# Layer 0's q, k, v projections by one level of Strassen's scheme, bias tables fetched for each head, normalising and the residual copy on ScalarE

## The chip, the cores and the metric

The kernel runs on one core of one Trainium2 chip. The metric is the device time of one execution in microseconds. A core has five engines that run beside each other, each with its own queue in order: TensorE (PE; its weight loads are shown apart, as PEld), VectorE (DVE), ScalarE (ACT), GpSimd (POOL) and SyncE (SP), which here only issues transfers.

## The reference, cut to what matters

The input x has shape (T, B, N, D) = (4, 8, 512, 512): T time steps, B images, N tokens and D features. Four layers follow each other, each as x = x + layer(groupnorm(x)). Layers 1 to 3 are convolutions; the change leaves them alone. Layer 0 is spiking attention with H = 8 heads of 64 features:

```python
q = heads(lif(bn(x @ Wq.T, ...)))        # k and v in the same way
scores = einsum('tbhnd,tbhmd->tbhnm', q, k) * scale + bias_table[rel]
out = lif(einsum('tbhnm,tbhmd->tbhnd', scores, v))
out = lif(bn((out * gate_scale + gate_shift) @ Wp.T, ...))
# lif, over t:  v = v + (xt - v) / 2;  spike = v >= 1;  v = v * (1 - spike)
```

There is no softmax, so the kernel takes q (k^T v) for the first part of the scores and multiplies v with a table for each head for the second, where rel depends on n - m alone. All of q, k, v and the outputs are spikes, 0 or 1; x and the weights of the projections are f32.

## The kernel before, in words

**Steps.** layer0 (L254) goes through 32 steps, one for each (image b, time t), with t inside, since lif carries a state over t. Step n computes the projections of its (b, t); in the same pass of the loop (L754) stand the attention and the output projection of steps n - 2 and before. Attention is done for two steps at once, in every second pass.

**Projections.** project_in (L539) makes one 128 x 512 block in one PSUM bank: 4 f32 matmuls over the 4 chunks of 128 features. Each of v, k and q has 4 blocks, so a step has 12 blocks and 48 matmuls. For k and v the tokens are the partitions, for q the features. In the profile an f32 matmul is two instructions. VectorE then takes the block out of PSUM: potential (L511) adds half the state, L553 (k, v) or L502 (q) compares with 1 and writes spikes, L518 or L504 clears what has spiked. The constant of the batch norm is added to the state on GpSimd for v, k and the output projection (L519) and on ScalarE for q (L505). At the last t of an image the state isn't kept.

**The input.** x arrives in four transfers (load_quarters, L454, on SP's queue), is normalised in place by one VectorE operation over 128 x 2048 (L714), and transposed by VectorE in 32 x 32 blocks (L524). The statistics of the next groups are counted from other loads of x (xs, L468).

**Attention.** prepare_bias (L383) builds, once at the start, all tables of the heads in SBUF: 12 transfers with overlapping rows (hankel) on ScalarE's queue, each followed by a reversed ScalarE copy (L398). attend (L580) multiplies the spikes of v with these tables (biased, L590, 144 bf16 matmuls of 256 columns). It splits each table into a part that is shared by both halves of the tokens and two own parts: shared_part, then a ScalarE copy from PSUM to PSUM (L610) onto which own_part accumulates, then copies of halves of the partitions (L622), then q (k^T v) on top (L626) and the lif (neuron_o, L479).

**Output projection.** project_out (L644): ScalarE casts spikes to fp32r (L652), 8 fp32r matmuls (L655), potential, then for each half of the features a VectorE operation that compares and adds the residual x, read with a stride of four elements (L666), and statistics (L670). GpSimd copies the mirrored edges (L677) and starts the store (L682). The residual is loaded on SP's queue (xr, L450).

**What sets the order.** In layer 0 a planner orders each engine's instructions ahead of the run: by the place in the program, by readiness with its own costs, and by free buffers. `issue_after` puts named instructions behind another on its engine. PSUM has 8 banks; 7 (ps_mm) serve the projections, attention and the output projection. Layer 1 starts when the first image's table and rows have been loaded into the space of the weights (start_layer1, L729).

Of the kernel before, what the change touches and what calls it, by code (L numbers as in the profile page):

```python
# [41 lines left out]
ALU = mybir.AluOpType  # L42
# [31 lines left out]
LAG = 2  # L74
RING = W2_N + 2 * LAG + 5
# [6 lines left out]
def shape_constants():  # L82

    p = np.arange(P)
    block = (p[:, None] // DH == p[None, :] // DH).astype(np.float32)
# [168 lines left out]
def layer0(  # L254
# [5 lines left out]
    ps_mm = s.enter_context(tc.tile_pool(name="ps_mm", bufs=7, space=PSUM))  # L260
    ps_1 = s.enter_context(tc.tile_pool(name="ps_1", bufs=1, space=PSUM))
    wpool = s.enter_context(tc.tile_pool(name="w0", bufs=1))


    n_x1 = W1_N * X1_U
    wv = shared.tile([P, NC * D], F32, tag="v", name="w_v")
    wkq = shared.tile([P, max(2 * NC * D, n_x1)], F32, tag="kq", name="w_kq")
    wT = {
        n: w.rearrange("p (c d) -> p c d", c=NC)
        for n, w in (("v", wv), ("k", wkq[:, : NC * D]), ("q", wkq[:, NC * D : 2 * NC * D]))  # L270
    }
    eye = shared.tile([K1_P, SHIFTS, M1], F32, name="eye")


    c_twice = {n: wpool.tile([P, D], F32, name=f"c2_{n}") for n in "vkp"}
    toep = [wpool.tile([P, H, 3, N // 2 + P], BF16, name=f"toep_{j}") for j in range(3)]
# [5 lines left out]
    xp = s.enter_context(tc.tile_pool(name="x0", bufs=4))  # L282
    xqp = s.enter_context(tc.tile_pool(name="xq0", bufs=1))
    small0 = s.enter_context(tc.tile_pool(name="s0", bufs=4))
    x1p = s.enter_context(tc.tile_pool(name="x1p", bufs=2))
    state = s.enter_context(tc.tile_pool(name="state", bufs=1))
    work = s.enter_context(tc.tile_pool(name="work", bufs=1))


    def load_weights(n, engine):  # L290
        rows = i[f"wT_{n}"].rearrange("(q c a) e -> q a c e", c=NC, a=SQ)
        for q in range(P // SQ):
            engine.dma_start(wT[n][q * SQ : (q + 1) * SQ], rows[q])
# [4 lines left out]
    def batch_norms():  # L298
# [13 lines left out]
        )  # L312
        return op.ins

    def as_rows_of(cols, rows):

        n = cols.shape[1]
        ps = ps_mm.tile([n, P], F32, tag="mm", name="ps_rows")
        nc.tensor.transpose(ps, cols, ident)
        nc.scalar.copy(rows[:n], ps)  # L320
        return rows[:n]

    def rows_of():
        return work.tile([P, 2, P], F32, tag="kvb", name="rows", bufs=2)

    def along_free(rows, j):
# [4 lines left out]
        for c in range(NC):  # L331
            at = NC * j + c
            nc.tensor.matmul(
                ps[:, c * P : (c + 1) * P], lhsT=ident[:n, at : at + 1].to_broadcast([n, P]),
                rhs=rows, start=True, stop=True,
            )
# [5 lines left out]
    def prepare_in(n):  # L342
        j = "qkvp".index(n)
        scale = along_free(a_rows, j)
        for k in range(NC):
            nc.vector.tensor_mul(wT[n][:, k, :], wT[n][:, k, :], scale)
        return nc.scalar.mul(c_twice[n], along_free(c_rows, j), 2.0).ins

    n_h, n_u = N - 1, toep[0].shape[3]

    def split_bias():

        parts = tc.dram_tile([3, H * 3 * n_h], BF16, name="bias_parts")
# [13 lines left out]
        nc.vector.tensor_scalar_mul(own, own, math.sqrt(D))  # L367
# [5 lines left out]
        for x in range(3):  # L373
            nc.scalar.dma_start(
                bass.AP(
                    parts.tensor, parts.offset + x * n_h,
                    [[3 * n_h, H], [H * 3 * n_h, 3], [1, n_h]],
# [5 lines left out]
    def prepare_bias(parts):  # L383


        for h in range(0, H, 2):
            for z in range(3):
                hankel = state.tile(
                    [P, 6, n_u], BF16, tag="h_o" if (h + z) % 2 else "h_p", name="hankel"
                )  # L390
                nc.scalar.dma_start(
                    hankel,
                    bass.AP(
                        parts.tensor, parts.offset + (z * H + h) * 3 * n_h,
                        [[1, P], [n_h, 6], [1, n_u]],
                    ),
                )
                nc.scalar.copy(  # L398
                    toep[z][:, h : h + 2].rearrange("p h x u -> p (h x) u"), hankel[:, :, ::-1]
                )  # L400
# [8 lines left out]
    def prepare_out(wp_rows):  # L409
# [5 lines left out]
        for k in range(NC):  # L415
# [19 lines left out]
            nc.scalar.copy(wpT[1][:, k, :], wp)  # L435
        c = c_half[:, 3, :]
# [3 lines left out]
        rows = rows_of()[:, 0]  # L440
        nc.scalar.mul(
            c_twice["p"].rearrange("p (g v) -> p g v", g=PH),
            phases(along_free(as_rows_of(c, rows), 0)), 2.0,
        )
# [48 lines left out]
    def neuron_q(ps, c, t, spikes):  # L493

        a_col, c_col = a_half[:, 0, c : c + 1], c_half[:, 0, c : c + 1]
        h = h_of["q"][:, c, :]
        v = work.tile([P, N], F32, tag="v", name="v_q", bufs=2)
        if t == 0:
            nc.vector.tensor_scalar(v, ps, a_col, c_col, op0=ALU.mult, op1=ALU.add)
        else:  # L500
            nc.vector.scalar_tensor_tensor(v, ps, a_col, h, op0=ALU.mult, op1=ALU.add)
        nc.vector.tensor_scalar(spikes, v, 1.0, None, op0=ALU.is_ge)  # L502
        if t < T - 1:
            nc.vector.scalar_tensor_tensor(v, v, 1.0, v, op0=ALU.is_lt, op1=ALU.mult)  # L504
            nc.scalar.activation(h, v, AF.Identity, bias=c_col, scale=0.5)  # L505

    def potential(ps, n, c, t):

        before = c_twice[n] if t == 0 else h_of[n][:, c, :]
        v = work.tile([P, D], F32, tag="v", name=f"v_{n}", bufs=2)  # L510
        op = nc.vector.scalar_tensor_tensor(v, before, 0.5, ps, op0=ALU.mult, op1=ALU.add)  # L511
        potentials.append(op.ins)
        return v

    def keep(v, n, c, t):
        if t < T - 1:
            h = h_of[n][:, c, :]
            nc.vector.scalar_tensor_tensor(h, v, 1.0, v, op0=ALU.is_lt, op1=ALU.mult)  # L518
            nc.gpsimd.tensor_add(h, h, c_twice[n])  # L519

    def transposed(xt, k):

        xk = work.tile([P, N], F32, tag="xn", name="xn", bufs=5)
        nc.vector.transpose(  # L524
            xk.rearrange("p (j s) -> p j s", s=SQ), xt[:, :, k * SQ : (k + 1) * SQ]
        )
        return xk

    def new_spikes():
# [3 lines left out]
            "q": work.tile([P, NC, 2, N], F16, tag="q", name="q"),  # L533
            "v": work.tile([P, NC, H, 2, DH], F8, tag="vtok", name="vtok"),
            "both": work.tile([P, 2, H, 2, DH], F8, tag="both", name="both"),
# [3 lines left out]
    def project_in(n, c, xn, got, t):  # L539

        ps = ps_mm.tile([P, D], F32, tag="mm", name="ps_in")
        cut = slice(c * P, (c + 1) * P)
        for k in range(NC):
            lhsT, rhs = (wT["q"][:, k, cut], xn[k]) if n == "q" else (xn[k][:, cut], wT[n][:, k, :])
            mm = nc.tensor.matmul(ps, lhsT=lhsT, rhs=rhs, start=k == 0, stop=k == NC - 1)  # L545
        if n == "q":
# [945 lines left out]
```

## Time and profile before

| | us |
|---|---|
| median of 3 runs | 2823.92 |
| lowest, highest | 2821.92, 2826.72 |
| the profiled execution | 2823.14 |
| its span, first to last instruction | 2821.3 |
| first projection matmul of layer 0 | 22.15 |
| first matmul of layer 1's convolution | 1959.36 |

The page of the profile has for every engine the busy time, for every group of instructions (a line, an engine, an operation and its tiles) the count, busy time, mean duration of one in ns, and the idle time just before it with what ended it. A table of stretches gives busy times by window with TensorE's granted clock, the DMA share and GB/s. A timeline gives single instructions with their start and duration in us. Matmuls overlap in the records, so their mean duration is longer than their pace.

| engine, 420 to 660 us | busy us of 240 |
|---|---|
| TensorE | 238.20 |
| VectorE | 197.64 |
| ScalarE | 46.98 |
| GpSimd | 85.67 |

### The profile page before, as it was taken

The page shows a single profiled execution, that of the slowest core. Times are in us where ns is not written, and L with a number is a line of the kernel's source. Part 1 is how long each engine was busy: PE and PEld are TensorE (multiplying, and loading weights), DVE is VectorE, ACT ScalarE, POOL GpSimd, SP SyncE. Part 2 cuts the span into 40 slices and gives each one's busy share as a digit, 9 for nine tenths or more (in the row PEclk, how much of TensorE's full clock was granted, in tenths as well). Part 3 has the DMA queues.
Part 4 walks back from the last instruction along what each step waited for, and adds up shares of the span by engine and source line. Part 5 has one row for each costly group of instructions (what it writes and reads, how often), then busy time and mean ns, then how long its engine had stood idle before and what let it go on. Part 6 is the DMA issues. An engine that isn't in the chain of part 4 may idle for free. (4 is left out here: it accounts for less than half of the span.)

```text
span 2821.3 us, 46325 instructions
## 1 busy us (share of the span) xinstructions
PE 2723.7 (97%) x17558; PEld 1402.5 (50%) x17558; DVE 2061.0 (73%) x3686; ACT 718.0 (25%) x1145; POOL 939.4 (33%) x2144
## 2 busy tenths in 40 slices
PE   7899999999999999999999999999899999789999
PEld 3455555554555555555555555555233333334447
DVE  7787978878788787977878778786565555665550
ACT  1422020221202112022220312202111121366663
POOL 2132433324243242433325324243211111354440
PEclk9899999999999999999999999999999999889999
DMA  6523223232232322323222121113877777667755
GB/s 169 149 77 76 75 71 82 61 76 72 65 91 61 76 69 64 87 61 83 64 65 61 46 69 46 50 63 93 215 204 207 209 214 208 152 177 210 216 170 149
DMA packets 326547, 314.03 MB, mean 111 GB/s; under 512 B 20691, under 2 KB 245771, under 8 KB 326211
## 3 DMA queue, kind: packets, MB, share of 16 engines
q1 hardware_dynamic: 258144, 228.59, 32.6%
q0 software_dynamic: 16448, 51.27, 4.8%
q10 hardware_dynamic: 51731, 31.20, 3.9%
q8 instruction: 138, 2.26, 0.4%
q14 instruction: 86, 0.70, 0.1%
HBM read 207.31 MB, written 103.67 MB: 110 GB/s over the span
## 5 line engine op out<-in xcount | busy, mean ns | idle before, releaser
L545 PE MATMUL ps_in<-w_v,xn 128*128 128x512 f32 x1024 | 465.0, 600 | 13.8 <-DVE xn L524 8.5
L930 PE MATMUL ps_conv<-x,bt 112*64 112x512 f32 x2048 | 449.5, 595 | 17.5 <-DMA x<-x 13.9
L545 PE MATMUL ps_in<-w_kq,xn 128*128 128x512 f32 x1024 | 452.9, 594 | 0.0
L545 PE MATMUL ps_in<-xn,w_kq 128*128 128x512 f32 x1024 | 450.1, 595 | 0.0
L677 POOL COPY x1s<-x1s 128x2 f32<-128x2 f32 (+1 forms) x1024 | 221.5, 271 | 356.8 <-DVE x1s L666 342.7
L545 PEld LDWEIGHTS ps_in<-w_v,xn 128*128 128x128 f32 x1024 | 193.3, 192 | 232.3 <-issue 202.3
L655 PE MATMUL ps_out<-wp,so 128*128 128x512 f32 x1024 | 306.2, 442 | 1.3 <-ACT so L652 1.3
L545 PEld LDWEIGHTS ps_in<-xn,w_kq 128*128 128x128 f32 x1024 | 193.7, 190 | 226.6 <-issue 219.7
L545 PEld LDWEIGHTS ps_in<-w_kq,xn 128*128 128x128 f32 x1024 | 194.4, 190 | 219.4 <-issue 205.9
L930 PEld LDWEIGHTS ps_conv<-x,bt 112*64 112x64 f32 x2048 | 146.6, 136 | 309.7 <-issue 290.6
L652 ACT CAST so<-so 128x512 fp32r<-128x512 fp8e4 x128 | 78.7, 618 | 808.5 <-PE ps_out L655 783.0
L519 POOL TENSOR_TENSOR h_v<-h_v,c_v 128x512 f32<-128x512 f32 x96 | 134.4, 1400 | 449.7 <-DVE h_v L518 326.8
L655 PEld LDWEIGHTS ps_out<-wp,so 128*128 128x128 f32 x1024 | 192.5, 188 | 93.7 <-issue 56.4
L1370 PE MATMUL ps_conv<-x,band_t 32*32 32x512 f32 x6144 | 230.2, 597 | 1.3 <-ACT o L1410 1.3
L666 DVE SCALAR_TENSOR_TENSOR x1s<-v_p,xr 128x256 f32<-128x256 f32 x256 | 180.3, 744 | 17.1 <-DMA x<-x1s 8.4
L937 ACT ACTIVATE xo<-ps_conv,off 128x512 f32<-128x512 f32 x128 | 87.8, 687 | 393.9 <-PE ps_conv L930 329.7
L952 POOL DMA_DIRECT2D x<-xo x128 | 71.6, 566 | 338.0 <-ACT xo L937 329.7
L595 PE MATMUL ps_own<-toep,vtok 128*128 128x256 bf16 x1536 | 180.7, 272 | 3.5 <-ACT ps_own L610 3.5
L1265 DVE SCALAR_TENSOR_TENSOR x<-ps_conv,inv,x 128x512 f32<-128x512 f32 x128 | 95.1, 749 | 103.6 <-PE ps_conv L1229 91.6
L595 PEld LDWEIGHTS <-vtok 128*128 128x128 fp8e4 x1536 | 149.4, 98 | 30.8 <-issue 8.7
L505 ACT ACTIVATE h_q<-v_q,c_half 128x512 f32<-128x512 f32 x96 | 69.2, 721 | 373.3 <-DVE v_q L504 373.3
L519 POOL TENSOR_TENSOR h_k<-h_k,c_k 128x512 f32<-128x512 f32 x96 | 123.8, 1290 | 107.6 <-DVE h_k L518 104.8
(196 smaller groups left out, 3647.0 us busy)
## 6 DMA issues: line engine op xcount, KB each, us to landing
x<-x SPq DMA_DIRECT2D x64, 917.0 KB
x<-x1s POOLq DMA_DIRECT2D x128, 262.0 KB, 2.7
xq<-in_x SPq DMA_DIRECT2D x128, 256.0 KB
xr<-in_x SPq DMA_DIRECT2D x128, 256.0 KB
out<-o SPq DMA_DIRECT2D x120, 256.0 KB
xs<-in_x SPq DMA_DIRECT2D x112, 256.0 KB
x<-x SPq DMA_DIRECT2D x128, 224.0 KB
x<-xo ACTq DMA_DIRECT2D x128, 128.0 KB
```

What stands on the lines that cost most here:

```text
L519: nc.gpsimd.tensor_add(h, h, c_twice[n])
L545: mm = nc.tensor.matmul(ps, lhsT=lhsT, rhs=rhs, start=k == 0, stop=k == NC - 1)
L595: nc.tensor.matmul(out, lhsT=src[:, c, h, :], rhs=toep[z][:, h, x, u : u + half], start=start and c == 0 and z == 0, stop=c == 1 and z == ...
L652: nc.scalar.copy(tokens, so[:, :, t % 2, c * P : (c + 1) * P])
L655: nc.tensor.matmul(ps, lhsT=tokens[:, k, :], rhs=wpT[z][:, k, :], start=k == 0 and z == 0, stop=k == NC - 1 and z == 1,)
L666: nc.vector.scalar_tensor_tensor(own, v.rearrange("p (g v) -> p g v", g=PH)[:, two, :], 1.0, by_phase[:, two, :], op0=ALU.is_ge, op1=ALU.add,)
L677: nc.gpsimd.tensor_copy(x1[:, f, u : u + n], x1[:, fm, um - n + 1 : um + 1][:, ::-1])
L930: mm = nc.tensor.matmul(ps[q * M1 : (q + 1) * M1, :], lhsT=bt[:, z, :], rhs=xt[:, w0 : w0 + N_PS1, z : z + NV], start=z == 0, stop=z == SH ...
L937: nc.scalar.activation(xo[:, a, :], ps, AF.Identity, bias=off[:, t : t + 1])
L952: engine.dma_start(bass.AP(dst.tensor, dst.offset + (q * n_half * W1_OUT * B + b) * D + f * NV, [[B * D, W1_OUT], [W1_OUT * B * D, n_half] ...
L1265: nc.vector.scalar_tensor_tensor(inner, ps, w["inv"], x, op0=ALU.mult, op1=ALU.add, accum_out=sums[:, 0, :] if summed else None,).ins
L1370: mm = nc.tensor.matmul(ps[c * QP : (c + 1) * QP, :], lhsT=band[g * QP : (g + 1) * QP, int(last), dx, :], rhs=src[:, dx : dx + PH, :], sta ...
```

## The change

**Products.** Tokens, features and outputs are each cut in two halves. Instead of 8 products of quarters, 7 products of sums of quarters are made (Strassen's scheme in Winograd's form), and the four result quarters are sums of products. k and v are done together: `unit("kv", cc)` makes blocks of 128 tokens by 256 columns of k and 256 of v; `unit("q", 0)` does q with 256 tokens for two feature chunks. A step has three units: two for k and v, one for q. Sums of products are formed in PSUM: a bank gets a ScalarE copy of another and later products accumulate on it. One product (the seventh) is doubled by ScalarE into SBUF and added to the state on GpSimd.

```diff
+    def product(kind, cc, x, n, ps, start=False):
+        w, x = w_of[n], x[n]
+        for kk in range(2):
+            if kind == "kv":
+                mm = nc.tensor.matmul(
+                    ps, lhsT=x[:, kk, cc * P : (cc + 1) * P], rhs=w[:, :2, kk, :],
+                    start=start and kk == 0, stop=kk == 1, skip_group_check=True,
+                )
+        for c in range(2) if kind == "q" else ():
+            for kk in range(2):
+                mm = nc.tensor.matmul(
+                    ps[:, c, :], lhsT=w[:, 2, kk, c * P : (c + 1) * P], rhs=x[:, kk, :],
...
+        a = new("a")
+        yield mul(a, 1, True)
+        g = new("g")
+        mul(g, 7, True)
+        b = new("b")
+        seeds.append(nc.scalar.copy(b, a).ins)
+        twice = work.tile([P, 2, HN], F32, tag="twice", name="twice")
+        nc.scalar.mul(twice, g, 2.0)
+        for o in range(2):
+            h, c, _ = of(1, o)
+            nc.gpsimd.tensor_add(h, c if t == 0 else h, twice)
+        yield
+        mul(b, 6)
+        yield
+        e = new("e")
+        seeds.append(nc.scalar.copy(e, b).ins)
+        mul(a, 2)
+        evict(a, 0, 0)
+        yield
+        mul(b, 5)
+        yield
+        f = new("f")
+        seeds.append(nc.scalar.copy(f, b).ins)
+        mul(e, 4)
+        evict(f, 1, 1)
+        evict(e, 1, 0)
+        yield
+        mul(b, 3)
+        evict(b, 0, 1)
+        yield
```

**Evictions.** evict adds half the state on VectorE as before. For k and v the threshold is now two operations of 256 columns, which write 2^-6 in place of 1; for q it stays one. GpSimd adds the constant for k and v; for q ScalarE does, in two pieces of 256 columns.

```diff
+            op = nc.vector.scalar_tensor_tensor(
+                v, c if t == 0 and half == 0 else h, 0.5, ps, op0=ALU.mult, op1=ALU.add
+            )
...
+                    nc.vector.tensor_scalar(
+                        out, own, 1.0, SPIKE, op0=ALU.is_ge, op1=ALU.mult, saturate=False
+                    )
...
+                nc.vector.scalar_tensor_tensor(h, v, 1.0, v, op0=ALU.is_lt, op1=ALU.mult)
+                nc.gpsimd.tensor_add(h, h, c)
+            else:
+                nc.vector.scalar_tensor_tensor(v, v, 1.0, v, op0=ALU.is_lt, op1=ALU.mult)
+                for k in range(2):
+                    nc.scalar.activation(
+                        h[:, k], v[:, k], AF.Identity, bias=c_q[:, 2 * o + k : 2 * o + k + 1]
+                    )
```

**Sums of the input and of the weights.** Each step needs four sums of quarters of x, on GpSimd; the weights are summed once at the start, on VectorE, after they have been scaled.

```diff
+    def sum_x(n, part):
+            if part == 0:
...
+                eng.tensor_add(x[5], x[7], x[4])
+                eng.tensor_sub(x[7], x[1], x[7])
+            else:
+                eng.tensor_sub(x[6], x[5], x[1])
+                eng.tensor_sub(x[3], x[2], x[6])
+    def sum_weights(first, end):
...
+        nc.vector.tensor_sub(t3, b22, b12)
+        nc.vector.tensor_sub(t1, b12, b11)
+        nc.vector.tensor_sub(t2, b22, t1)
+        nc.vector.tensor_sub(b12, b21, t2)
```

**Tables.** The tables of all heads no longer lie in SBUF. For each attention the tables are fetched on SP's queue, for each head one shared (128 x 3 x 384 bf16) and one own (128 x 2 x 3 x 384 bf16). Four heads of each kind are held; they are fetched in the pass before, the others as the first come free. The rows come unreversed; instead q and the output spikes are read in reverse.

```diff
+    def fetch(kind, n=1):
+        first, n_x = (0, 1) if kind == "x" else (1, 2)
+        for h in order[kind][:n]:
+            table = tables.tile([P, n_x, 3, n_u], BF16, tag=f"t_{kind}", name=f"table_{kind}")
+            nc.sync.dma_start(
...
+                table = held["x"].pop(0)
+                biased(common[j][:, two, :], both, 2 * j + two, table[:, 0], two == 0)
+            if 2 * j + HEADS_HELD < H:
+                fetch("x", 2)
...
+            if h + HEADS_HELD < H:
+                fetch("own")
```

**Normalising and the residual.** Four ScalarE operations of 128 x 512 normalise x, with r and -m r as columns. In project_out ScalarE copies the residual, by halves, into the output tile, behind the last seed; VectorE then adds in place, contiguously.

```diff
-                nc.vector.tensor_scalar(flat, flat, m, r, op0=ALU.subtract, op1=ALU.mult)
+            for xt in as_rows(xs[n]):
+                nc.scalar.activation(xt, xt, AF.Identity, bias=shift, scale=r)
...
+            with tc.issue_after(seeds[-1]):
+                op = nc.scalar.copy(halves[z][1], by_phase[:, two, :])
...
             nc.vector.scalar_tensor_tensor(
-                own, v.rearrange("p (g v) -> p g v", g=PH)[:, two, :], 1.0,
-                by_phase[:, two, :], op0=ALU.is_ge, op1=ALU.add,
+                own, v.rearrange("p (g v) -> p g v", g=PH)[:, two, :], 1.0, own,
+                op0=ALU.is_ge, op1=ALU.add,
             )
```

**Order.** A step is now a row of 21 slots (7 for each unit). The output projections stand at slots 3, 6, 10 and 13, the normalising of the next step at 13, its transposes at 14 and 17, its sums at 18 and the end, k^T v at 16. The residual's loads stand ahead of the attention, no longer after it. add_halves adds the bytes of two spikes as one 16-bit integer. Seven matmuls with one row of constants are put ahead of everything.

```diff
+    outs = (3, 6, 10, 13)
...
+            if slot == 13 and n <= last:
                 add_halves(spikes, steps[n][1])
+                normalise(n + 1)
+            if slot == 14:
+                transpose(n + 1, 0)
+                if n % 2 == 0 and done >= 0 or n == 1:
+                    fetch("x", HEADS_HELD)
+                    fetch("own", HEADS_HELD)
...
+            if slot == 17:
+                transpose(n + 1, 1)
+            if slot == 18:
+                sum_x(n + 1, 0)
```

## The prediction

> **What bounds the kernel now.** I read the table of stretches first, to see which engine is full while layer 0 runs, and then the groups by cost.
>
> ```profile
> core 0: us, PE busy (x) PEld busy (x) DVE busy (x) ACT busy (x) POOL busy (x), PEclk, DMA share, GB/s
> 420.00:540.00 120.00, 119.55 (x450) 66.38 (x449) 98.49 (x161) 20.89 (x36) 41.66 (x96) 1.00 0.28 74
> 540.00:660.00 120.00, 118.65 (x450) 65.82 (x449) 99.16 (x175) 26.09 (x44) 44.01 (x90) 1.00 0.27 70
> ```
>
> TensorE is busy 99% at full clock, VectorE 82%, ScalarE 20%, GpSimd 36%. Layer 0 is TensorE-bound: only fewer TensorE cycles shorten it, and only until another engine is full. Its work, and what GpSimd does beside it:
>
> ```profile
> L545 PE MATMUL ps_in<-w_v,xn 128*128 128x512 f32 x1024 | 465.0, 600 | 13.8 <-DVE xn L524 8.5
> L545 PE MATMUL ps_in<-w_kq,xn 128*128 128x512 f32 x1024 | 452.9, 594 | 0.0
> L545 PE MATMUL ps_in<-xn,w_kq 128*128 128x512 f32 x1024 | 450.1, 595 | 0.0
> L519 POOL TENSOR_TENSOR h_v<-h_v,c_v 128x512 f32<-128x512 f32 x96 | 134.4, 1400 | 449.7 <-DVE h_v L518 326.8
> ```
>
> An f32 matmul appears as two instructions: 16 matmuls per projection and step, 32 steps, 1024 records. The 600 ns overlap; the pace is read from the weight loads, one for each instruction:
>
> ```profile
> 601.28 0.19 PEld L545 LDWEIGHTS ps_in<-xn,w_kq 128*128 128x128 f32 x1 [0.24 <-issue]
> 601.71 0.19 PEld L545 LDWEIGHTS ps_in<-xn,w_kq 128*128 128x128 f32 x1 [0.24 <-issue]
> 602.14 0.19 PEld L545 LDWEIGHTS ps_in<-xn,w_kq 128*128 128x128 f32 x1 [0.24 <-issue]
> ...
> 641.44 1.70 PEld L655 LDWEIGHTS ps_out<-wp,so 128*128 128x128 f32 x8
> ```
>
> One f32 instruction of 512 columns takes 0.43 us (starts 0.43 apart). Eight fp32r instructions' weight loads of 0.188 cover 1.70: starts (1.70 - 0.19)/7 = 0.216 apart. So a 0.19 us load hides under a 0.216 us matmul. The projections cost 96 x 0.43 = 41.3 us a step. A pair of steps with its attention takes 118.5 us (the projection of v that follows the k,v product starts at 447.80 and at 1751.98, 11 pairs later).
>
> The third reading is VectorE against GpSimd:
>
> ```profile
> 52.38 0.68 DVE L511 SCALAR_TENSOR_TENSOR v_k<-c_k,ps_in 128x512 f32<-128x512 f32 x1
> ...
> 52.55 1.27 POOL L519 TENSOR_TENSOR h_k<-h_k,c_k 128x512 f32<-128x512 f32 x1 [2.01 <-DVE h_k L518]
> 53.10 1.00 DVE L553 TENSOR_SCALAR k<-v_k 128x512 fp8e4<-128x512 f32 x1
> ```
>
> The operation that reads PSUM runs beside GpSimd's addition at 0.68. The threshold after it takes 1.00 where its free time is 0.43: it waits until the addition ends at 53.82.
>
> [...]
>
> **The change, part by part.** The sum is made against the profiled execution: 2823.1 us, its span 2821.3, the other 1.8 taken as constant. It lies 0.8 below the median 2823.92.
>
> *Products.* A unit has 7 products of two 512-column matmuls, or for q of four 256-column ones. Two k-v units: 2 x 7 x 2 x 2 = 56 instructions x 0.43 = 24.1 us. One q unit: 56 instructions of 256 columns; none is in the trace, the nearest row of that length is fp32r's 0.216: 12.1 us. Together 36.2 for 41.3: 5.15 us a step, **165 us** over 32 steps. Bounds of the q pace: half of 0.43 (0.215, nothing gained)[...]. Fully exposed, 0.40, is excluded by the 0.216.
>
> *Seeds.* Products accumulate on copies of earlier ones, so TensorE now waits for ScalarE: three PSUM-to-PSUM copies in a unit, nine a step. Each has one other product, 1.72 us, in between. The same kind of wait is in the trace: ps_x ends at 616.05, ScalarE's copy (L610) runs 616.09 to 616.66, ps_own starts at 616.78; with 0.16 of modelled matmul tail, 0.89 us. So 0.83 us of room: one other ScalarE operation in front (0.4 to 0.8) is covered, two are not. ScalarE has per pair 23.2 now, plus 18 seeds x 0.57, 6 doublings x 0.61, 8 normalisings (0.80 by the page), [...]and q's state in 256-column pieces (12 x 0.49 for 6 x 0.72): 52 us of 108, 48%. Queued behind a late ScalarE operation are the next seed and so TensorE. I take 0.5 us a step, 16 us; ends 0 and 0.4 a seed (115).
>
> *VectorE.* Per pair: normalising leaves, -2 x 1.34; the halves' sum on half the elements, -0.7; the residual addition reads contiguous data, 16 x (0.74 - 0.42) = -5.1; k's and v's thresholds in two pieces, 32 x 0.29 for 16 x 0.43, +2.5. Sum -6.1. GpSimd gets 6 state additions and 4 input sums a step: 320 instructions to the 288 of L519. The 288 cost VectorE now, by mean over free time in three rows, 128 x ((0.998 - 0.426) + (0.616 - 0.426) + (0.668 - 0.427)) = 128 us, 0.45 each. 20 more a pair: +8.9. VectorE goes from 97.6 to 100.4 us, of 108.2 instead of 118.5: 93%. GpSimd: 42.3 + 20 x 1.27 = 68, 63%. Neither exceeds TensorE, but the room for lateness shrinks: a state addition late on GpSimd holds the eviction that reads it, VectorE's queue behind that, and then PSUM banks. I take 0.5 us a step, 16 us; ends 0 and 1.5 (48).
>
> *Tables.* 12 fetches and 12 ScalarE copies (2.11 each) leave the start; each of 16 attentions fetches 8 x (288 + 576) KB = 7.1 MB: 113 MB, about 65 GB/s more on SP's queue, DMA share from 0.28 to about 0.5. Half is held ahead. The other 3.5 MB must come while attention runs, 17.7 us (614.58 to the last ps_own at 632.27). The start's stretch 65:70 moved 338 GB/s, 85:90 292, 60:65 97: at 300 it is 12 us. It fits, with little room, and xr and xq loads share the queue; a fetch that waits for its slot holds those behind it. I take 0.5 us an attention, 8 us; ends 0 and 6 (96).
>
> *The start.* Both k's and v's weights must be scaled and summed ahead of the first full unit[...]; the first product slips from 22.15 to about 25, and waits between the first ones add some us. Against that, TensorE is busy 144 of the 158 us from 22 to 180, with a gap of 5 us at 70 while table fetches fill the DMA; this cover is lighter afterwards. Net 0, ends -10 and +10.
>
> *At nothing:* reversed reads of q and of the spikes (ScalarE's reversed copy L398 moves 2304 elements in 2.11[...]; for the matmul unshown, at worst 8 x 0.35 a pair, 45 us, held unlikely); the shift of the mean (0.2 on VectorE, hidden by its idle time); the added one-row matmuls ahead of the start (TensorE waits for inputs until 22). Layers 1 to 3 (from 1959 on) are untouched.
>
> **Sum.** -165 + 16 + 16 + 8 + 0 = -125; 2823.1 - 125 = 2698. The tails above make it 2658 (no stall) to about 2735.
>
> **Rivals.**
> *Seeds late.* Two ScalarE operations stand in front of many seeds. For: ScalarE's work doubles, in order, with operations that wait for VectorE among it. Against: 48%, and 0.83 us of room. At 0.4 us a seed: 2823 - 165 + 115 + 24 = 2797 with the small terms at what I took; half of it 2740.
> *Tables late.* Attention waits for its last three tables, 6 us each time: 2823 - 165 + 96 + 32 = 2786. For: 17.7 us for 3.5 MB. Against: the prefetch, and 300 GB/s.
> [...]VectorE outgrows TensorE. Without any waits it has 97.6 - 8 - 6.1 = 83.5 us a pair (8 = 128/16); with 38 additions at s each, 83.5 + 38 s. It matches today's 118.5 at **s = 0.92**; beyond, the kernel is slower. At a full lock, 1.27, it is 132 us, 16 x 13.3 = 213 us slower; midway, s = 1.05, 123.4: 16 x 4.9 = +78, 2901. For: GpSimd's additions now come in twos, and most VectorE operations have two SBUF inputs. Against: 0.45 measured, and operations on PSUM and statistics run beside it.
> *The 7/8 isn't had:* q's short matmuls don't halve. Excluded above[...].
>
> **How the numbers follow.** Likeliest case 0.58: 2698 (its own range 2658 to 2740). Seeds late 0.15, tables late 0.10: both still faster.[...] Balance near zero 0.03. About 0.2% (5.6 us) is what a measurement of this kernel can tell from no change. Faster 0.83, same 0.03, slower 0.14. The range from 2658 reaches over the two middle rivals to 2800[...].
>
> **What would show it.** Right: TensorE over 95% busy in layer 0's stretches, a pair near 111 us, q's instructions 0.216 apart, VectorE near 92%, L553's successor with means not far over 0.5. Wrong: waits of matmuls for the seeds' copies (seeds), for DMA (tables), or for VectorE with VectorE over 97%[...]. Layer 1 starting within 10 us of 1959 - 125 = 1834 tests that all of it lies in layer 0.

## The result and the profile after

| | before | after |
|---|---|---|
| median of 4 runs, us | 2823.44 | 2911.61 |
| span of the profiled execution, us | 2821.3 | 2908.5 |
| mean granted TensorE clock | 0.987 | 0.966 |
| TensorE, VectorE, ScalarE, GpSimd busy, us | 2723.7, 2061.0, 718.0, 939.4 | 2656.9, 2142.4, 1166.5, 1319.5 |

The ratio after to before is 1.0315, 95% interval 1.0297 to 1.0334: slower by 88 us, where 125 faster was forecast. All of it lies in layer 0: the first convolution matmul of layer 1 starts at 2060.76, before at 1959.36, 101 later (1834 was forecast), and 14 of those come back afterwards. First the table of stretches, after; its columns are busy us (and instructions) of TensorE, weight loads, VectorE, ScalarE and GpSimd, then granted clock, DMA share and GB/s.

```profile
420.00:540.00 120.00, 110.68 (x470) 72.28 (x469) 99.45 (x173) 49.12 (x86) 63.79 (x109) 0.96 0.47 126
540.00:660.00 120.00, 107.58 (x459) 71.34 (x458) 101.12 (x183) 49.73 (x91) 67.33 (x113) 0.96 0.45 114
```

TensorE fell from 99% to 91% busy, and its clock with it; VectorE stands at 84%, not at the 93% forecast, ScalarE at 41% and GpSimd at 55%. No engine is full. A pair of steps takes 125.0 us (the first product of the second step starts at 583.04 and 11 pairs later at 1958.51) where the prediction counted 108.2 for TensorE's own work. So TensorE waits, in gaps. That q's instructions are not what is slow shows in one of its products (line, operation, count, least, median and longest duration in ns, first and last start):

```profile
L545 PE MATMUL ps_q_b<-x_sum,w_raw x8: 379/379/380, 581.3 to 582.8; 128*128 128x256 f32 x8
```

Eight starts from 581.3 to 582.8, 0.21 apart. In the groups by cost, the projections of k and v have idle time now, where those of before had 0.0 in two of three rows:

```profile
L539 PE MATMUL ps_kv_b<-w_sums,x_sum 128*128 128x512 f32 x512 | 264.6, 643 | 61.6 <-issue 61.1
...
L539 PE MATMUL ps_kv_a<-w_raw,x_raw 128*128 128x512 f32 x512 | 257.5, 622 | 19.8 <-DMA xq<-in_x 9.6
```

The gaps of one pair, from the timeline of TensorE (start, length, the instructions, and in brackets the idle time ahead of them and what ended it):

```profile
574.00 0.55 PE L649 MATMUL ps_kv<-v,k 128*128 128x128 fp8e4 x7 [1.80 <-DVE v L584]
...
583.04 1.88 PE L539 MATMUL ps_kv_a<-w_raw,x_raw 128*128 128x512 f32 x4
585.10 1.98 PE L539 MATMUL ps_kv_g<-w_sums,x_raw 128*128 128x512 f32 x4 [0.18 <-POOL x_raw L851]
591.27 2.96 PE L539 MATMUL ps_kv_b<-w_sums,x_sum 128*128 128x512 f32 x4 [4.18 <-issue]
...
639.66 2.55 PE L671 MATMUL ps_own<-table_own,v 128*128 128x256 bf16 x12 [4.12 <-ACT ps_own L690]
```

Two gaps of over 4 us, one as a step ends and one as attention begins. The label "issue" of the first is a wait of which the profile names no releaser: `ps_kv_b` is a bank that ScalarE seeds with a copy of `ps_kv_a` (L609). `ps_kv_a` was done at 584.9; the copy ran at 590.60, and the matmul followed it at 591.27. What ScalarE did till then, and VectorE and GpSimd with it, is the core of this case. ScalarE first:

```profile
585.63 0.91 ACT L597 ACTIVATE h_q<-v_q,c_q 128x256 f32<-128x256 f32 x2 [5.27 <-DVE v_q L595]
588.78 1.91 ACT L597 ACTIVATE h_q<-v_q,c_q 128x256 f32<-128x256 f32 x4 [2.24 <-DVE v_q L595]
590.60 0.57 ACT L609 COPY ps_kv_b<-ps_kv_a 128x512 f32<-128x512 f32 x1
```

ScalarE idles 5.27 and 2.24 us, waiting for VectorE (L595) with q's state pieces (L597), and the seed stands behind these in its queue. VectorE:

```profile
580.52 3.41 DVE L588 TENSOR_SCALAR q<-v_q 128x512 fp8e4<-128x512 f32 x1
583.96 1.63 DVE L595 SCALAR_TENSOR_TENSOR v_q<-v_q 128x512 f32<-128x512 f32 x1
585.52 0.67 DVE L576 SCALAR_TENSOR_TENSOR v_q<-h_q,ps_q_f 128x512 f32<-128x512 f32 x1
...
587.53 1.15 DVE L595 SCALAR_TENSOR_TENSOR v_q<-v_q 128x512 f32<-128x512 f32 x1
```

A threshold of 0.43 us (L588) takes 3.41, the operation after it 1.63 instead of 0.69. L576, which reads one operand from PSUM, takes its free 0.67. And GpSimd:

```profile
579.15 1.29 POOL L774 TENSOR_TENSOR h_p<-h_p,c_p 128x512 f32<-128x512 f32 x1
580.38 2.04 POOL L614 TENSOR_TENSOR h_q<-c_q,twice 128x512 f32<-128x512 f32 x2
582.37 1.26 POOL L850 TENSOR_TENSOR x_sum<-x_raw 128x512 f32<-128x512 f32 x1
583.71 1.34 POOL L851 TENSOR_TENSOR x_raw<-x_raw 128x512 f32<-128x512 f32 x1
585.01 1.72 POOL L853 TENSOR_TENSOR x_sum<-x_sum,x_raw 128x512 f32<-128x512 f32 x1
586.81 1.33 POOL L854 TENSOR_TENSOR x_sum<-x_raw,x_sum 128x512 f32<-128x512 f32 x1
```

Seven additions all but back to back; six of them the change has added (two of the doubled product, four input sums). VectorE's threshold began at 580.52 and ended at 583.93, after three of them. L595 ended at 585.60, and the addition that began at 585.01 (L853) took 1.72 where L850 took 1.26: it seems that GpSimd can be held as well. Before, nearly all such additions came singly (253 of 255 from 200 to 1900 us), and a threshold of k lost 0.57 on average. And a gap costs more than its length. The same table for two stretches, one ahead of the seed's arrival and one behind it:

```profile
586.00:591.30 5.30, 1.12 (x4) 0.25 (x2) 5.16 (x9) 2.83 (x7) 2.06 (x2) 1.00 0.09 13
591.30:596.00 4.70, 4.70 (x7) 1.95 (x8) 0.29 (x1) 3.12 (x7) 2.49 (x2) 0.64 0.00 0
```

First VectorE works 5.16 of 5.30 us and TensorE 1.12; then TensorE works throughout, at a granted clock of 0.64, and VectorE 0.29. They take turns: an engine with 16% of idle time is what the other waits for. Behind the gap of 4.12 at 639.66 the clock is 0.60 (639.70 to 644.00). It is lower, too, behind the two short gaps of 0.53 and 1.80 us around the k,v product:

```profile
571.00:574.50 3.50, 1.17 (x18) 1.00 (x16) 3.47 (x8) 0.57 (x1) 1.57 (x2) 1.00 0.00 0
574.50:583.00 8.50, 8.50 (x33) 7.19 (x33) 8.46 (x13) 0.57 (x1) 7.37 (x14) 0.80 0.31 81
```

TensorE was busy 1.17 of 3.50 us there, and the clock behind it was 0.80; the matmuls of `ps_q_a` there (574.4 to 576.9) have a median of 0.634 us, those of `ps_q_e` (579.6 to 581.1) 0.379. Over the 11 pairs TensorE idles 12.1 us a pair (busy 1242.7 of 1375.5); the remaining 4.7 or so of the 16.8 are slower matmuls, as the mean clock of 0.96 over 113 busy us (4.5) also says. The prediction had no term for the clock.

### The profile page after: what moved, and what is told of

Read it like the earlier page. It is cut to its first block, busy times and chain, and to the rows that moved or that the text cites. A ratio compares the mean times of both kernels' runs of the same rounds, so it can differ in the third digit from the quotient of the medians.

```text
span 2908.5 us, 50142 instructions
## 1 busy us (share of the span) xinstructions
PE 2656.9 (91%) x18092; PEld 1533.8 (53%) x18092; DVE 2142.4 (74%) x3939; ACT 1166.5 (40%) x1997; POOL 1319.5 (45%) x2464
## 5 line engine op out<-in xcount | busy, mean ns | idle before, releaser
L593 POOL TENSOR_TENSOR h_kv<-h_kv,c_kv 128x512 f32<-128x512 f32 x192 | 248.1, 1293 | 243.1 <-DVE h_kv L592 239.2
L539 PE MATMUL ps_kv_b<-w_sums,x_sum 128*128 128x512 f32 x512 | 264.6, 643 | 61.6 <-issue 61.1
L539 PE MATMUL ps_kv_a<-w_raw,x_raw 128*128 128x512 f32 x512 | 257.5, 622 | 19.8 <-DMA xq<-in_x 9.6
L671 PE MATMUL ps_own<-table_own,v 128*128 128x256 bf16 x1536 | 188.7, 279 | 48.2 <-ACT ps_own L690 45.4
L614 POOL TENSOR_TENSOR h_kv<-h_kv,twice 128x512 f32<-128x512 f32 x96 | 127.0, 1339 | 221.5 <-ACT twice L611 221.4
L584 DVE TENSOR_SCALAR k<-v_kv 128x256 fp8e4<-128x256 f32 x256 | 200.2, 782 | 5.9
L671 PEld LDWEIGHTS <-v 128*128 128x128 fp8e4 x1536 | 152.6, 100 | 87.4 <-issue 64.1
L539 PEld LDWEIGHTS ps_kv_b<-w_sums,x_sum 128*128 128x128 f32 x512 | 101.4, 201 | 173.1 <-issue 165.9
L744 ACT CAST so<-so 128x512 fp32r<-128x512 fp8e4 x128 | 78.8, 617 | 262.5 <-PE ps_out L747 260.2
L706 ACT COPY ps_f<-ps_own 64x512 f32<-64x512 f32 x256 | 142.9, 558 | 87.6 <-PE ps_own L671 82.8
L761 ACT COPY x1s<-xr 128x256 f32<-128x256 f32 x256 | 156.7, 664 | 20.5 <-DMA x<-x1s 17.0
L597 ACT ACTIVATE h_q<-v_q,c_q 128x256 f32<-128x256 f32 x192 | 87.0, 500 | 192.7 <-DVE v_q L595 188.1
```

Of the source, the lines that this page charges most:

```text
L539: mm = nc.tensor.matmul(ps, lhsT=x[:, kk, cc * P : (cc + 1) * P], rhs=w[:, :2, kk, :], start=start and kk == 0, stop=kk == 1, skip_group_c ...
L584: nc.vector.tensor_scalar(out, own, 1.0, SPIKE, op0=ALU.is_ge, op1=ALU.mult, saturate=False)
L593: nc.gpsimd.tensor_add(h, h, c)
L614: nc.gpsimd.tensor_add(h, c if t == 0 else h, twice)
L671: nc.tensor.matmul(out, lhsT=src[:, c, h].rearrange("p t e -> p (t e)"), rhs=table[:, z, u : u + HN], start=start and c == 0 and z == 0, s ...
L706: nc.scalar.copy(final[j][a][two * DH : (two + 1) * DH, :], rows[a * DH : (a + 1) * DH, :])
```

## The experiments

**Theory A:** the added additions on GpSimd hold VectorE at the step's end; ScalarE, whose queue is in order, waits for VectorE, TensorE for ScalarE. **Rivals:** ScalarE's order alone (seeds late whatever GpSimd does); matmuls and evictions waiting for the additions' results; a capacity bound, VectorE's sum as the prediction's rival with the stall s had it. Each kernel is the one after with the edit shown, unless said otherwise; ratios are to the kernel before on the same chip, whose median is 2822 to 2823. Gains are differences of medians, over chips where the runs were not in one batch.

### q's state leaves ScalarE's queue

```diff
-                nc.vector.scalar_tensor_tensor(v, v, 1.0, v, op0=ALU.is_lt, op1=ALU.mult)
-                for k in range(2):
-                    nc.scalar.activation(
-                        h[:, k], v[:, k], AF.Identity, bias=c_q[:, 2 * o + k : 2 * o + k + 1]
-                    )
+                nc.vector.scalar_tensor_tensor(h, v, 1.0, v, op0=ALU.is_lt, op1=ALU.mult)
+                pending.append((h, o))
...
+        if kind == "kv" and cc == 0:
+            with tc.issue_after(seeds[-1]):
+                add_c_q()
```

add_c_q has ScalarE add q's constant in place, behind the first seed of the next step.

> Whole computation. VectorE writes q's kept state straight into the state, and ScalarE adds q's constant in place behind the first seed of the next step, no longer ahead of it. Theory (a chain: a run of six GpSimd additions holds VectorE's q evictions, ScalarE's q state waits for these, and the next seed or attention copy stands behind it in ScalarE's order): the waits of 4.2 us on the first ps_kv_b and of 4.1 us on the first ps_own of each pair go, with the slower clock behind them (about 1.8 and 1.0): 11 us a pair, 15 pairs, 2912 - 165 = about 2750. Rival (capacity: [...]the sum of VectorE's work sets the pace): the order on ScalarE is beside the point, 2900 to 2915.

Measured 2834.09, ratio 1.0049 (1.0031 to 1.0066): 78 faster than the kernel after, half of what the chain theory wanted and far more than capacity allows; VectorE is busy 88% there (1501.19 us from 200 to 1900), so 84% was no bound. The waits of TensorE, from 200 to 1900 us (sum, times, longest), in this kernel:

```profile
PE ps_kv L649 <- DVE v L584: 32.9, 21, 2.4
PE ps_kv_b L539 <- ACT ps_kv_e L619: 18.1, 16, 1.6
PE ps_kv_g L539 <- POOL x_raw L859: 17.5, 13, 2.9
PE ps_x L671 <- DVE v_q L576: 17.4, 7, 3.2
```

The "issue" wait (57.0 in the kernel after, the longest 4.2) is gone; `ps_x` now waits 17.4 for banks that VectorE hasn't emptied (L576). VectorE is still late, and the next in the queue shows it.

### The four input sums: left out, or on VectorE

Left out (the products read unsummed inputs):

```diff
...
-                eng.tensor_add(x[5], x[7], x[4])
-                eng.tensor_sub(x[7], x[1], x[7])
...
-                eng.tensor_sub(x[6], x[5], x[1])
-                eng.tensor_sub(x[3], x[2], x[6])
+                x[5], x[6], x[3] = x[4], x[1], x[2]
```

> Leaves out the four sums of quarters of x in each step; the products take plain quarters. Theory (chain): the run of six GpSimd additions at the end of a step shrinks to two, VectorE's q evictions are some 4 us earlier, so the seed and the attention copy are nearly in time: 2750 to 2800. Rival (capacity): 128 additions fewer, each worth the mean stall of 0.58 us: 2912 - 74 = 2838.

Measured 2804.45, ratio 0.9938 (0.9924 to 0.9953): 107 faster, just above the chain theory's upper end. Made on VectorE instead (`eng = nc.vector`):

> Whole computation; the four sums of x are made by VectorE, not GpSimd. Theory (chain): the long GpSimd run that holds VectorE goes, VectorE itself gets 4 x 0.69 us a step ahead of q's evictions; these are late by about 2 us less than now: 2810 to 2870. Rival (capacity): VectorE's total stays as it was (128 x 0.69 more, 128 x 0.58 of stalls less): 2912 +- 15.

Measured 2902.12, ratio 1.0288 (1.0271 to 1.0306): 9 faster: none of the gains the chain theory named, and inside the range of the capacity rival (2912 +- 15). By itself this run speaks for that rival; the two before it speak against it. Taken together: an addition that GpSimd makes at this point costs the kernel about as much as if VectorE made it.

### The k,v product four slots later

```diff
-            if slot == 16 and n <= last and n % 2 == 0:
+            if slot == 20 and n <= last and n % 2 == 0:
```

> Whole computation; k^T v is put at slot 20, the end of the step, in place of slot 16. Theory: its wait for VectorE's v thresholds (0.5 + 1.8 us in each pair, and 1.7 of slower clock behind it) goes: 16 x 4 = 64, about 2850. Rival (capacity): VectorE is as late as before, the wait only moves: 2905 to 2915.

Measured 2905.85, ratio 1.0298 (1.0282 to 1.0313): 6 faster, in the range that the rival gave (2905 to 2915), and not the theory's 2850. The wait of 1.80 at 574.00 was not a cause; the lateness moved to the next matmul (`ps_kv_g` waits 4.43 us for an input sum).

### None of the added additions, with and without stand-ins

The first kernel leaves out all 320 (at the first time step VectorE copies c into the state). The second makes as many, at the same places, into buffers that nobody reads:

```diff
         for o in range(2):
...
-            nc.gpsimd.tensor_add(h, c if t == 0 else h, twice)
...
+            nc.gpsimd.tensor_add(nobody(), twice, twice)
...
+                x[5], x[6], x[3] = x[4], x[1], x[2]
-                eng.tensor_add(x[5], x[7], x[4])
+                eng.tensor_add(nobody(), x[7], x[4])
...
```

> Leaves out all the additions that the change gives to GpSimd: the four input sums of a step, and the six additions of the doubled product to the kept state (at the first time step VectorE copies c into the state instead). The products read unsummed inputs; seeds, doublings, evictions and their order stay. Theory A, the loss of 16.8 us a pair of steps comes from VectorE being held by those additions at the step's end: without them nearly all of it returns, 2908 - 16 x (12 to 16.8), that is 2640 to 2720. Theory B, the seeds' place behind q's state pieces in ScalarE's queue costs by itself, whatever GpSimd does: no more than about as without the input sums alone (2804), so 2760 or more, with TensorE still waiting some us a step for the seed of kv_b.

> As the run without GpSimd's added additions, but GpSimd makes as many additions of the same size at the same places into buffers that nobody reads; no matmul and no eviction waits for their results (products read unsummed inputs and the kept state lacks the doubled product, as in that run). If each addition costs[...]: all of the loss comes back, 2880 to 2915. If the loss is that matmuls and evictions wait for the additions' results: it stays near 2717, up to 2750. Between the two, the split is read off.

Measured without them: 2716.85, ratio 0.9614 (0.9598 to 0.9630), 195 faster than the kernel after and in theory A's range. With the stand-ins: 2951.15, ratio 1.0455 (1.0440 to 1.0471), above its range of 2880 to 2915. So 320 additions whose results nobody needs cost 234 us. That settles it against both rivals that need no hold: seeds and ScalarE's order are the same in both kernels, and nobody waits for a result (with the stand-ins, VectorE waits 6.8 us for GpSimd from 200 to 1900, all for statistics; TensorE and ScalarE don't wait for it). q's threshold by its durations (ns: min, median, max), in the first and in the second kernel:

```profile
L588 DVE TENSOR_SCALAR q<-v_q x128: 379/427/430, 80.9 to 1818.8; 128x512 fp8e4<-128x512 f32 x128
```

```profile
L588 DVE TENSOR_SCALAR q<-v_q x128: 380/428/7661, 84.8 to 2048.9; 128x512 fp8e4<-128x512 f32 x128
```

Without the additions no threshold of q exceeds 0.43 us; with them one took 7.66. The mean is 0.43 without them, 1.91 with the stand-ins and 1.23 in the kernel after, where the run has pauses of 0.08 us ahead of two of the sums; that is likely why the stand-ins cost 39 us more. k's thresholds (L584), which stand by other additions, are held about as much without the added ones (means 0.76 and 0.79 us from 200 to 1900, shortest 0.25): what the change added falls mostly on q's, at the step's end. The timeline of the second kernel shows the threshold of 7.66 us, VectorE first and then GpSimd:

```profile
1023.48 0.65 DVE L576 SCALAR_TENSOR_TENSOR v_q<-h_q,ps_q_a 128x512 f32<-128x512 f32 x1
1024.16 7.66 DVE L588 TENSOR_SCALAR q<-v_q 128x512 fp8e4<-128x512 f32 x1
1031.75 0.67 DVE L576 SCALAR_TENSOR_TENSOR v_q<-h_q,ps_q_f 128x512 f32<-128x512 f32 x1
```

```profile
1023.39 1.28 POOL L776 TENSOR_TENSOR h_p<-h_p,c_p 128x512 f32<-128x512 f32 x1
1024.62 2.03 POOL L616 TENSOR_TENSOR nobody<-twice 128x512 f32<-128x512 f32 x2
1026.61 1.26 POOL L853 TENSOR_TENSOR nobody<-x_raw 128x512 f32<-128x512 f32 x1
1027.84 1.25 POOL L854 TENSOR_TENSOR nobody<-x_raw 128x512 f32<-128x512 f32 x1
1029.06 1.26 POOL L856 TENSOR_TENSOR nobody<-x_raw 128x512 f32<-128x512 f32 x1
1030.29 1.25 POOL L857 TENSOR_TENSOR nobody<-x_raw 128x512 f32<-128x512 f32 x1
```

Seven additions run without a pause from 1023.39 to 1031.54, and the threshold, issued during the first, ends at 1031.82. It did not get in between any two: it was held for the whole run, not for one addition.

### The run broken up

The stand-ins again, but the four at the step's end are spread over the slots of the output projections:

```diff
+            if slot in (3, 6, 10, 13) and n <= last:
+                nc.gpsimd.tensor_sub(nobody(), xns[n][2], xns[n][1])
```

> As the run with ten additions a step into buffers that nobody reads, but the four that stood in for the input sums at the step's end follow, one at a time, the state additions of the k, v units. The same number of additions, no run of six any more. If each addition costs by itself (0.6 us of VectorE wherever it stands): within 30 of that run, 2920 to 2980. If a run of additions costs more than its parts because VectorE doesn't get in between two of them: 2740 to 2850.

Measured 2880.12, ratio 1.0205 (1.0190 to 1.0221): 71 faster with the same number of additions, which falls between the two expectations. They did not come singly, as was meant: in the trace 62 of the 128 directly follow another of them and 49 the doubled product's stand-ins, so runs of up to five remain where there were seven. So of the 234 us, 71 net belong to the place of four additions in a longer run, and 163 stay (0.51 us for each of the 320); this is no price of a lone addition.

### Normalising and residual copies

Back on VectorE in the kernel after, and alone on ScalarE in the kernel before:

```diff
-            for xt in as_rows(xs[n]):
-                nc.scalar.activation(xt, xt, AF.Identity, bias=shift, scale=r)
+            flat = xs[n].rearrange("p j f -> p (j f)")
+            nc.vector.tensor_scalar(flat, flat, r, shift, op0=ALU.mult, op1=ALU.add)
...
-                op = nc.scalar.copy(halves[z][1], by_phase[:, two, :])
```

> Undoes one part: the normalising and the residual copies go back to VectorE, all else as changed. They take 2 x 1.34 and about 5.1 us a pair of steps from VectorE's relief. Theory A (VectorE late at the step's end): slower by some 60 to 120, 2970 to 3030. Theory B (ScalarE's ordered queue is what is late, and these copies lengthen it): 2912 or less.

> The kernel before with one part of the change alone: normalising and the residual copies on ScalarE. There TensorE is 99% busy in layer 0, so VectorE's 7.8 us a pair are worth nothing: 2817 to 2829. If VectorE's lateness costs already in the kernel before: 2810 or less. If ScalarE's queue delays the attention's copies: 2835 or more.

Measured 2962.61, ratio 1.0489 (1.0473 to 1.0505), 51 slower than the kernel after, a little under theory A's 60 to 120 and on its side; and 2831.51, ratio 1.0030 (1.0021 to 1.0040), 9 slower than before, between two of the ranges expected. The relief is worth 51 us where VectorE is late and less than nothing where it isn't. In the kernel before with this part alone, the wait of projections for VectorE's transposes grew from 1.1 to 11.0 us; that the normalising on ScalarE, ahead of those transposes, is the cause is likely and was not tried apart.

### q by the plain eight products

Four banks, no seeds and no doubled product for q, k and v as changed; then the same with q's state deferred as in the first experiment.

```diff
+        if kind == "q":
+            for k in range(2):
+                for half in range(2):
+                    for o in range(2):
+                        op = product(kind, cc, x, n_w, banks[half, o], k == 0, n_x)
+                        if k == 1:
+                            evict(banks[half, o], half, o)
...
```

> Whole computation; k and v by 7 products, q by the plain 8 (four PSUM banks, no seeds, no doubling, no addition of the doubled product for q). TensorE has 1.73 us more a step, 55 in all; two of the ten added GpSimd additions of a step and 3 of 9 seeds go, all of them near the step's end. Theory A', the loss sits in the chain at the step's end, where q's seeds and doublings meet the input sums and the next seed: pair 111.7 plus 2 to 5 us, so 2908 - 16 x (8 to 11), 2730 to 2780, faster than before the change. Theory C, the loss goes with the number of GpSimd's additions (0.58 us each): 4 of 38 a pair fewer, 2.3 us a pair, set against nothing else: 2870 or more.

> As the run with q by 8 products, and in addition q's kept state is written straight from VectorE, its c added by ScalarE behind the next step's first seed (the edit of the first experiment). If the seed behind q's state pieces is what remains, 10 to 60 below that run, 2690 to 2760; if the lateness was q's seeds or the input sums, within 10 of it.

Measured 2887.09, ratio 1.0219 (1.0204 to 1.0235), and 2811.40, ratio 0.9955 (0.9941 to 0.9970). The first is where theory C, the number of additions, wanted it: 55 us more of TensorE and still 25 faster. The second is 76 faster than the first, as deferring was alone (78) and more than the 60 expected at most, and just ahead of the kernel before. The guess that q's own seeds were most of the lateness fell.

### c of k and v on TensorE, a version that beats both

GpSimd's largest group is not new: `h + c` for k and v, 192 additions. They go, and 32 of the doubled product at first time steps become copies (the expectation's 256 and 64 are miscounted; its sum uses the 192). c is the same for all tokens, so a matmul of ones with c's three bf16 parts can put it into the bank (ones of 96 x 128 by c of 96 x 512; the second call adds the other half's c, less the first's):

```diff
+        add_c(a, 0, True)
-        yield mul(a, 1, True)
+        yield mul(a, 1, kind == "q")
...
+        add_c(b, 1, False)
         mul(b, 5)
...
-                nc.gpsimd.tensor_add(h, h, c)
```

> Whole computation; the c of k and v is no longer added to the kept state by GpSimd (256 additions of 512 elements go, 64 small copies come) but by two one-row-block bf16 matmuls a unit into the products' PSUM banks (128 of 0.216 us, 28 us of TensorE). If GpSimd's additions cost by holding VectorE, 0.58 us each, wherever they stand in the step: 192 fewer in the steps that keep state are 111 us of VectorE; with the 28 added, 2790 to 2870. If only the run of six additions at the step's end costs (those stay): 2900 to 2945.

> The run before in this batch with c on TensorE, and in addition q's kept state written straight from VectorE, its c added behind the next step's first seed (the edit of the first experiment, worth 78 there). If both act on different parts of the lateness: 2730 to 2790, faster than before the change. If they act on the same part: within 20 of the better of the two alone, 2815 to 2855.

Measured 2829.82, ratio 1.0029 (1.0017 to 1.0041): 82 faster than the kernel after, where 192 x 0.58 - 28 = 83 was the sum. These additions stand all over the step, so their number counts too. With q's state deferred: **2758.75, ratio 0.9774 (0.9760 to 0.9789)**. Together the two edits gain 153, of 82 + 78 apart. Its table of stretches:

```profile
420.00:540.00 120.00, 115.27 (x503) 74.86 (x502) 103.78 (x182) 51.48 (x91) 55.72 (x111) 1.00 0.48 135
540.00:660.00 120.00, 115.28 (x518) 76.41 (x517) 103.25 (x201) 56.51 (x103) 48.78 (x98) 1.00 0.48 131
```

TensorE is 96% busy at full clock, with VectorE at 86%, more than in the kernel after. Two further steps from there, one addition fewer in the run at the step's end, and q by eight products:

> The run with c on TensorE and q's state deferred (2759), and the fourth input sum, not needed until the next unit's seventh product, issued in that unit's fourth slot. The run at the step's end becomes five additions instead of six. If the length of the run decides: 5 to 30 faster, 2730 to 2754. If the number: within 5 of 2759.

> The run with c on TensorE and q's state deferred (2759), with q by 8 products. TensorE has 55 us more; q's two additions leave the run at the step's end (six to four). If the length of the run is most of what is left over TensorE's own time (2759 - 2640 - 28 = 91): 2700 to 2745. If not: 2750 to 2815.

Measured 2758.77, ratio 0.9780 (0.9766 to 0.9795), and 2782.71, ratio 0.9871 (0.9854 to 0.9888). Neither gains. The first edit did not shorten the run: in its trace the fourth sum (L886) still starts 0.08 us behind the third in 26 of 32 steps, as it did in 25 without the edit, so this run says nothing about length. In the second TensorE idles 39 us from 200 to 1900 instead of 72, so of q's eighth product's 55 us a net 24 remain; whether fewer additions or fewer seeds saved the rest was not tried apart.

## Why the prediction was wrong, step by step

The balance, from the runs: 2823 - 165 (products) + 59 (what the kernel without the added additions has over that) + 195 (the added additions) = 2912.

- *Products, -165:* right, as far as the runs show (with the pace of 0.216 that it took, the sum gives 163). q's instructions are 0.21 apart, and the kernel without the added additions runs at 2717 although it keeps all seeds, doublings and tables. The 59 that it has over 2658 are about TensorE's added idle time: 72.8 us from 200 to 1900, before 9.2.
- *Tables, +8:* right in kind. All waits of TensorE for table fetches sum to 2.4 us.
- *The start, 0:* right. The first projection's matmul slips to 33.27 instead of the 25 forecast, but attention first starts at 138.86, before at 139.7.
- *Seeds, +16:* as a cost of their own about right. In the kernel without the added additions TensorE waits 23.7 us for `ps_kv_b`'s seeds from 200 to 1900, and 15.4 for the attention's copies (`ps_own`), before 3.1. ScalarE is busy 53.4 us a pair (586.88 in 11), where 52 was forecast: the doubling (L611) takes 0.60 us for the 0.61 assumed, q's pieces (L597) 0.50 for 0.49, the residual copy (L761) 0.66, a price for which the author had an estimate that no run showed. The tail of 0.16 stands: four of `ps_kv_a`'s instructions take 1.88 in the record, 4 x 0.43 + 0.16. The reason given for the small size was wrong in its place, though. "Two are not" counted ScalarE operations by their own length; the six that stand ahead of the seed at a step's end take 0.47 each, but idle 7.5 us for VectorE. That VectorE is in ScalarE's chain was named only in passing, under the rival.
- *VectorE and GpSimd, "I take 0.5 us a step, 16 us; ends 0 and 1.5 (48)":* **the step that failed.** It measured 195. Two errors in it. A mean over additions that came singly, 0.45, was carried to additions placed six in a row, where a single threshold takes 3.41 in place of 0.43. The mean itself hardly moved: the three rows behind the 0.45 leave out the residual's addition, held as well (L666, mean 0.744, median 0.620); with it the kernel before has (128 + 256 x 0.124) / 288 = 0.56, and the mean over the stalled groups after is 0.58. (So the contiguous read saved less, too: L767 has the 0.42 taken as its median, 0.419, but a mean of 0.596. The thresholds in two pieces, taken at 0.29, have medians of 0.281 for v and 0.552 for k.) And the test was a sum, 100.4 of 108.2 us, as though room anywhere in the pair could absorb a stall. The one path it named, an eviction waiting for a late state addition, isn't in the trace: VectorE waits for none there. VectorE is held where q's last evictions, ScalarE's next seed and the attention's first copy all hang on it, and stands at 0.29 of 4.7 us right after. With VectorE at 84%, TensorE idles 12.1 us a pair.
- *At nothing:* right for the reversed reads: a matmul of `ps_f` has 0.379 us at the median before (L626) and after (L714), the cast of the output spikes 0.617 in both (L652, L744). The shift of the mean takes 0.16 (L814).
- *What isn't in the sum:* the granted clock behind the gaps, some 4.5 us a pair, about 72 in all. From 420 to 660 it is 0.96 in the kernel after, and 1.00 in the one without the added additions (longest wait for a seed from 200 to 1900 2.3 us) and in the best version (1.6 us). The trace of the kernel before had such a drop already: 0.50 from 75 to 80 us, behind a gap of 7.39 us.
- *The rivals:* the one with the stall s, where VectorE outgrows TensorE, had the right pair of engines, but not the right condition: it was to decide from s = 0.92; measured was 0.58, with VectorE not full. That its 2901 at s = 1.05 lies near 2912 is chance. Its chance, the 0.14 of "slower", rested on that condition, and was too small for it. "Seeds late" is how it shows, not its cause.
- *"Wrong: waits ... for VectorE with VectorE over 97%":* this sign would have missed it. The waits carry other names (issue, ScalarE), and VectorE's busy share is 84%. The signs for right did fail: TensorE 91%, a pair of 125.0, and k's threshold (L584) at a mean of 0.78, not 0.5.

Held in the trace above were a threshold (L588, 3.41 us for 0.43) and an operation with two SBUF inputs (L595, 1.63 for 0.69). Not held were L576, with one input in PSUM (0.67 amid the run), and statistics: one of the kernel after (L497 at 1049.44) ran its usual 0.69 inside an addition on GpSimd (L593, 1049.04 to 1050.31). What in the hardware decides this was not shown, and other forms of the threshold were not tried.

## What to carry to other kernels

Work given to an engine that can hold another up is priced by where it stands: look at what runs in a row, what the held engine owes at that moment, and who queues behind that. A sum of busy times says whether an engine can be the bound, not whether it will be waited for; with engines that hang on each other in turn, 84% was late enough. Before a bound is lightened, list the operations whose lateness it hid, and take work off the engine that holds first: here the scheme, with c of k and v added by TensorE and q's state out of ScalarE's way, is 63 us faster than the kernel before, and without them 88 slower.

## What the runs showed of the hardware that was not expected

- A VectorE threshold held through a whole run of GpSimd additions: 7.66 us for 0.43.
- Who is held varies. In the run of seven each stand-in for an input sum took 1.25 to 1.26 us and VectorE bore the loss; in the kernel after the third sum (L853) took 1.72 in the median; where it is shown above, VectorE's L595 ended in its first 0.6 us.
- TensorE's granted clock fell to 0.80 behind gaps of only 0.53 and 1.80 us.
- ScalarE's residual copy, 256 elements read at a stride of four, takes 0.66 us on average (0.64 to 0.71) where q's contiguous pieces of 256 elements (L597) take 0.50. That the stride is the reason was not tried.
